# The output projection of a group by Strassen's seven products, and weights in rings of blocks

## The chip, the cores and the metric

The kernel runs on one core of a Trainium2 chip. The metric is the device time of one execution in microseconds (us), as the median of several runs. A profile is one execution, recorded instruction by instruction. The engines are TensorE (PE; its weight loads are shown as PEld), VectorE (DVE), ScalarE (ACT), GpSimd (POOL) and SyncE (SP). SP and POOL issue the transfers (DMA) here. Matmuls write into PSUM; the kernel uses eight banks of it, four for projections and output products, two for scores, two for the attention products.

## The reference

The input x has 8 sequences of 256 tokens with 512 features, in float32, as everything is.

```python
xn = layernorm(x)
q = rope(xn @ wq.T)            # 32 heads of 128
k = rope(xn @ wk.T)            # 8 key/value heads, each used by 4 query heads
v = xn @ wv.T
scores = q @ k.T / sqrt(128)   # scaled by key for later query rows, then causal
s = concat_heads(softmax(scores) @ v) @ wo.T       # (256, 4096) @ (4096, 512)
g = silu(top-2 of 4 low-rank experts of xn)
out = x + s * g
```

## The kernel before

The tokens are worked in NTB = 4 token blocks of two sequences (512 tokens, b = 0 and 1). A token block has eight groups g, one for each key/value head with its four query heads. A *step* is one group of one token block (32 steps), a *unit* one group of one sequence (64 units).

**Projections.** q, k and v are made in *quads*: 512 output features by 512 input features for both sequences, by Strassen's method in the form of Winograd: seven products of half-size blocks in place of eight. A product is a `piece` of `quad`, four matmuls of 256 columns (eight instructions in the profile, since a float32 matmul is two). Its weight operand is one of the four blocks A11, A12, A21, A22 or of their sums S1 to S4, its other operand a block or a sum of the activations (XB, XT). The products go into three PSUM banks (pa, pd, pe) and are put together by VectorE and ScalarE, which keep intermediate values in "side" tiles. There are twelve quads a token block.

`load_weights` brings the weights of a quad. In the first token block it loads the four blocks, VectorE forms the three further sums and S3 (S3 takes the place of A21), and POOL writes all seven to a scratch tensor in DRAM; later blocks read all seven from there in one transfer. The tile of seven blocks has two buffers.

**Attention.** `softmax` of a unit makes scores with TensorE, exponentials with ScalarE and normalising with VectorE, in one buffer p; VectorE transposes 32 by 32 blocks, and a bounce through DRAM (spread, then gather: `there`, `pT`, issued by SP) completes the transposition. `values` multiplies pT with v: av, for a half t of the query rows and all four heads, 512 columns wide. ScalarE copies it to aT.

**Output.** `load_out_weights` brings the 512 by 512 part of wo of a group, one tile of two buffers. `out_project` makes, for each t, `po`: four matmuls of 512 columns (one for a head), then VectorE adds the bank to the sum s of that row block (the first group copies). After the last group `finish` multiplies by the gate, adds x and stores. The gates are made by `experts` early in each token block and stay in four tiles.

**Order.** The program is written as jobs with engines, estimated durations, predecessors and buffers (*holds*). TensorE's jobs are laid in an order that weaves the quads of the next step with the scores of a step, the attention products of two units before (LAG_V) and the output products of three units before (LAG_O). `Plan.run` then plays the jobs through with these estimates; on each engine the earliest due job that is ready and has its buffers goes first. The order it finds is the program's order on every engine, and each engine then keeps to it on the chip. A hold with turns (x, w, wo) is taken in the order in which it was asked for. The wait for a result, or for a buffer, stands at the head of the instruction that needs it, and all that is later on the same engine or the same issuing queue is behind it. All engine calls pass through one helper, so nearly every row of the profile names its line, L116; the tiles tell what a row is. The tile names: `paq`, `pdq`, `peq` are the three banks of a query quad (k and v for keys and values), `s` the sums of the output, `w` a quad's weights, `wo` the output weights.

Of the kernel before, what the change touches and what calls it, by code (L numbers as in the profile page):

```python
# [69 lines left out]
A11, A12, A22, S3, S1, S2, S4 = range(7)  # L70
A21 = S3
# [33 lines left out]
class InOrder:  # L105
# [15 lines left out]
    def __init__(self, tc):  # L121
        for name in ("tensor", "vector", "scalar", "gpsimd", "sync"):
            setattr(self, name, self.Engine(tc, getattr(tc.nc, name)))

# [124 lines left out]
def layer(ctx: ExitStack, tc: tile.TileContext, x, wquad, woT, raT, bT, table, out):  # L249
# [6 lines left out]
    four = pool("four", 4)  # L256
# [12 lines left out]
        store.tile([P, 7, 2 * 2 * P], F32, tag=f"sums{i}", name=f"sums{i}") for i in range(NQUAD)  # L269
    ]  # L270

# [5 lines left out]
    def hold(tag):  # L277
        return Hold(rooms[tag])

    for tag, n in dict(  # L280
        mm=4, sc=2, av=2, x=4, m=2, s=4, gates=4, side=3, w=2, wo=2, c=2, sw=2, qT=3, kk=3, v=3,
        z=2, p=1, blocks=1, pT=3, aT=4, X=1,
    ).items():
        rooms[tag] = Room(n, tag in ("x", "w", "wo"))
# [3 lines left out]
    gates, sums_of, acts, out_weights, weights, x_hold = {}, {}, {}, {}, {}, {}  # L288
# [3 lines left out]
    def norm(tb):  # L292
# [4 lines left out]
        xh = [hold("x") for _ in range(NT)]  # L297
# [4 lines left out]
        def load(t):  # L302
            xs[t] = four.tile([P, D], F32, tag="x", name=f"x{tb}_{t}")
            nc.sync.dma_start(out=xs[t], in_=x[bass.ds(tb * TB + t * P, P), :])
# [46 lines left out]
        issues = [add("sp", 0.3, lambda t=t: load(t), opens=[xh[t]]) for t in range(NT)]  # L351
# [13 lines left out]
        for t in range(NT):  # L365
            xn = add("dve", 0.4, lambda t=t: normalise(t), after=[done[t]], opens=[mh[t]], closes=[xh[t]])
# [17 lines left out]
    def load_weights(tb, quad, first):  # L384

        h = hold("w")
        n = f"{tb}_{quad}"
        box = {}
        flat = lambda i, j: sums[quad][:, i:j, :].rearrange("p i (c m) -> p i c m", c=2)

        def load():
            w = box["w"] = two.tile([P, 7, 2, 2 * P], F32, tag="w", name=f"w{n}")
            if tb:
                nc.gpsimd.dma_start(out=w, in_=flat(0, 7))
            else:
                (nc.sync if first else nc.gpsimd).dma_start(out=w[:, :4], in_=wquad[quad])

        def form(i):
            w = box["w"]
            a, b, c, op = (  # L400
                (A21, A22, S1, nc.vector.tensor_add),
                (S1, A11, S2, nc.vector.tensor_sub),
                (A11, A21, S3, nc.vector.tensor_sub),
                (A12, S2, S4, nc.vector.tensor_sub),
            )[i]
            op(w[:, c], w[:, a], w[:, b])

        def keep_sums():
            nc.gpsimd.dma_start(out=flat(0, 7), in_=box["w"])

        if tb:
            there = add(
                "pool", 0.7, load, opens=[h], after=[sums_of[quad]], lag=9.0
            )
            return box, h, [there] * 7
        there = add(
            "sp" if first else "pool", 0.7, load, opens=[h], after=first, lag=11.0 if first else 7.0
        )
        f1 = add("dve", 0.7, lambda: form(0), after=[there])
        f2 = add("dve", 0.7, lambda: form(1), after=[f1])  # L420
        f3 = add("dve", 0.7, lambda: form(2), after=[f1])
        f4 = add("dve", 0.7, lambda: form(3), after=[f2])
        sums_of[quad] = add(
            "pool", 0.7, keep_sums, after=[f3, f4], closes=[h], lag=7.0
        )
        return box, h, [there, there, there, f3, f1, f2, f4]

    def quad(tb, which, out, room, rows, name):
# [3 lines left out]
        wbox, wh, there = load_weights(tb, which, [] if len(weights) > 1 else begun)  # L432
# [8 lines left out]
        def product(bank, i, half, b, t, first):  # L441
            w = wbox["w"]
# [5 lines left out]
            for m in range(2):  # L448
                for c in range(2):
                    a, x_ = w[:, i, c, :], xb[:, c, :]  # L450
# [7 lines left out]
        def piece(bank, i, half, b, t, first, after):  # L458
# [4 lines left out]
                closes=[wh, x_hold[tb]],  # L463
# [15 lines left out]
        if not tb:  # L479
            sums_of[which].near = (p1, 0.0)  # L480
# [264 lines left out]
    def values(tb, g, b):  # L745
# [5 lines left out]
        def of(t):  # L751
            box = {}

            def work():
                v = vbox[b][:, :, bass.ts(g % G, HD)]
                av = box["av"] = ps_av.tile([P, G, P], F32, tag="av", name=f"av{n}_{t}")
                for k in range(t + 1):
                    nc.tensor.matmul(
                        av, lhsT=v[:, k, :], rhs=pbox["pT"][:, :, t + k, :], start=k == 0,
                        stop=k == t,  # L760
                    )

            def read():
                box["aT"] = four.tile([P, G, P], F32, tag="aT", name=f"aT{n}_{t}")
                nc.scalar.copy(box["aT"], box["av"])

            h, ah = hold("av"), hold("aT")
            av = add(
                "pe", 0.86 * (t + 1), work, after=[p_done] + v_done, opens=[h], closes=[ph, vh]
            )  # L770
            aT = add("act", 0.6, read, after=[av], opens=[ah], closes=[h], near=(av, 1.0))
            attn[tb, g, 2 * b + t] = box, ah, aT
            pieces.append(av)

        for t in range(2):
            of(t)
        return pieces


    def load_out_weights(tb, g):  # L780
# [312 lines left out]
```

## Time and profile before

| what | value |
|---|---|
| runs | 1411.73, 1414.01, 1414.49 us; median 1414.01 |
| the profiled execution | 1410.33 us, span 1408.5 us, 15988 instructions |
| PE, PEld | 1384.1 us (98%), 952.8 us (68%) |
| DVE | 951.4 us (68%) |
| ACT | 604.3 us (43%) |
| POOL | 57.7 us (4%) |
| DMA | 249.31 MB, 177 GB/s on the mean |

The span runs from the first to the last instruction of the profiled execution; the execution takes 1.8 us more. A row of the groups reads: line, engine, operation, output <- inputs, shape, count | busy us in total, mean ns of one | idle us of the engine just before them <- what ended it. In the list of waits a row is: who waited for whom, us in total, times, the longest. In a timeline a row is: start in us, us, engine, line, operation and count. Ends of matmuls are modelled, so their durations overlap and the distance from start to start is what one costs. A DMA row gives the queue that issues, count, size, and the median us from issue to landing.

### The profile page before, as it was taken

The page shows a single profiled execution, that of the slowest core. Times are in us where ns is not written, and L with a number is a line of the kernel's source. Part 1 is how long each engine was busy: PE and PEld are TensorE (multiplying, and loading weights), DVE is VectorE, ACT ScalarE, POOL GpSimd, SP SyncE. Part 2 cuts the span into 40 slices and gives each one's busy share as a digit, 9 for nine tenths or more (in the row PEclk, how much of TensorE's full clock was granted, in tenths as well). Part 3 has the DMA queues.
Part 4 walks back from the last instruction along what each step waited for, and adds up shares of the span by engine and source line. Part 5 has one row for each costly group of instructions (what it writes and reads, how often), then busy time and mean ns, then how long its engine had stood idle before and what let it go on. Part 6 is the DMA issues. An engine that isn't in the chain of part 4 may idle for free.

```text
span 1408.5 us, 15988 instructions
## 1 busy us (share of the span) xinstructions
PE 1384.1 (98%) x5360; PEld 952.8 (68%) x5360; DVE 951.4 (68%) x2566; ACT 604.3 (43%) x1559; POOL 57.7 (4%) x97
## 2 busy tenths in 40 slices
PE   6999999999999999999999999999999999999998
PEld 5866676667766677666776766766677766676653
DVE  5888677776677657577485765847767666665663
ACT  3444444453534435344443444435444344434521
POOL 1000000000000000000000000000000000000000
PEclk9999999999999999999999999999999999999999
DMA  5667556655465553554655554555546454454453
GB/s 217 231 225 257 193 184 230 234 172 167 154 209 171 172 160 128 184 190 161 194 181 179 153 165 152 184 174 166 158 164 227 162 171 143 153 199 127 135 157 97
DMA packets 71170, 249.31 MB, mean 177 GB/s; under 512 B 7920, under 2 KB 40688, under 8 KB 63408
## 3 DMA queue, kind: packets, MB, share of 16 engines
q1 hardware_dynamic: 53280, 115.37, 27.4%
q0 software_dynamic: 17056, 132.13, 25.7%
q8 instruction: 42, 0.69, 0.2%
q10 hardware_dynamic: 752, 0.80, 0.2%
q14 instruction: 40, 0.33, 0.1%
HBM read 171.72 MB, written 76.55 MB: 176 GB/s over the span
## 4 chain that ended last, share of the span: by engine, by line
PE 94%; DMA 4%; DVE 2%; SPq 0%; issue 0%; ACT 0%; DVEq 0%
PE po L116 29%; PE paq L116 15%; PE av L116 11%; PE sc L116 9%; PE pdq L116 8%; PE pav L116 4%; PE pak L116 4%; PE peq L116 4%; DMA there<-blocks 2%; PE pdv L116 2%; PE pdk L116 2%; DMA pT<-there 1%; PE dle L116 1%; PE lme L116 1%; PE pev L116 1%; PE pek L116 1%
## 5 line engine op out<-in xcount | busy, mean ns | idle before, releaser
L116 PE MATMUL po<-wo,aT 128*128 128x512 f32 x1024 | 463.8, 596 | 0.0
L116 PEld LDWEIGHTS po<-wo,aT 128*128 128x128 f32 x1024 | 188.9, 191 | 194.9 <-issue 192.7
L116 ACT ACTIVATE p<-z,least 128x256 f32<-128x256 f32 (+7 forms) x512 | 207.4, 407 | 163.7 <-DVE least L116 150.9
L116 DVE CUSTOM_DVE_ANT_0 z<-sc,tab 128x256 f32<-128x256 f32 (+7 forms) x512 | 136.4, 304 | 164.6 <-PE sc L116 147.2
L116 PE MATMUL av<-pT,v 128*128 128x512 f32 x384 | 188.0, 602 | 8.0 <-DMA pT<-there 8.0
L116 PEld LDWEIGHTS sc<-kk,qTq 128*128 128x128 f32 x1024 | 163.8, 191 | 43.1 <-issue 31.1
L116 PE MATMUL paq<-XT,w 128*128 128x256 f32 x768 | 183.4, 382 | 0.2 <-ACT u3q L116 0.2
L116 PE MATMUL sc<-kk,qTq 128*128 128x256 f32 (+7 forms) x1024 | 172.8, 302 | 0.0
L116 PEld LDWEIGHTS paq<-XT,w 128*128 128x128 f32 x768 | 143.6, 190 | 42.4 <-issue 24.0
L116 DVE TENSOR_TENSOR s<-s,po 128x512 f32<-128x512 f32 x112 | 76.6, 684 | 119.9 <-PE po L116 119.7
L116 ACT COPY aT<-av 128x512 f32<-128x512 f32 x128 | 74.6, 583 | 150.2 <-PE av L116 149.8
L116 ACT COPY swq<-cq 64x1024 f32<-64x1024 f32 x128 | 133.6, 1044 | 7.4 <-DVE qTq L116 5.1
L116 DVE STREAM_TRANSPOSE blocks<-p 128x1024 f32<-128x1024 f32 (+1 forms) x128 | 123.2, 967 | 0.5 <-issue 0.2
L116 DVE TENSOR_SCALAR p<-p,total 128x256 f32<-128x256 f32 (+7 forms) x512 | 117.2, 293 | 2.3
L116 PEld LDWEIGHTS av<-pT,v 128*128 128x128 f32 x384 | 72.6, 192 | 54.3 <-issue 41.8
L116 ACT ACTIVATION_READ_ACCUMULATOR p<-z,least 128x1 f32 x512 | 96.1, 188 | 0.0
L116 DVE TENSOR_TENSOR qTq<-cq,tab 128x1024 f32<-128x1024 f32 x64 | 78.1, 1220 | 22.3 <-ACT cq L116 22.3
L116 DVE TENSOR_TENSOR qTq<-qTq,swq 128x1024 f32<-128x1024 f32 x64 | 77.7, 1215 | 0.5
L116 DVE TENSOR_TENSOR swq<-swq,tab 128x1024 f32<-128x1024 f32 x64 | 77.9, 1217 | 0.0
L116 PE MATMUL paq<-XB,w 128*128 128x256 f32 x256 | 61.1, 381 | 0.0
L116 PEld LDWEIGHTS pdq<-XT,w 128*128 128x128 f32 x256 | 48.6, 190 | 18.5 <-issue 11.7
L116 PE MATMUL pdq<-XT,w 128*128 128x256 f32 x256 | 60.6, 379 | 0.0
(106 smaller groups left out, 1329.1 us busy)
## 6 DMA issues: line engine op xcount, KB each, us to landing
w<-sums POOLq DMA_DIRECT2D x36, 1792.0 KB, 7.7
there<-blocks SPq DMA_DIRECT2D x256, 192.0 KB, 3.3
pT<-there SPq DMA_DIRECT2D x64, 768.0 KB, 4.3
wo<-in_woT_dram POOLq DMA_DIRECT2D x32, 1024.0 KB, 9.2
sums<-w POOLq DMA_DIRECT2D x12, 1792.0 KB, 7.5
w<-in_wquad_dram POOLq DMA_DIRECT2D x10, 1024.0 KB, 5.1
x<-in_x_dram SPq DMA_DIRECT2D x16, 256.0 KB, 5.3
xf<-in_x_dram SPq DMA_DIRECT2D x16, 256.0 KB, 4.7
```

Of the source, the lines that this page charges most:

```text
L116: ins = what(*args, **kwargs)
```

## The change

Four things change.

1. The output product of a step (both sequences of a group) is done as a quad is: 2 by 2 blocks of the attention output (rows: sequences, columns: pairs of heads) with 2 by 2 blocks of the output weights (rows: pairs of heads, columns: halves of the 512 features), by seven products. `values` therefore makes av by pair of heads k, all 256 query rows in one tile, with matmuls of 256 columns. VectorE forms four sums of attention blocks in each step (`s` and, in place, `a` in the new names), and four sums of output weights in each step of the first token block.
2. Each of the seven products has a sum of its own, `acc` 1 to 7, over the eight groups. The first group copies with ScalarE, the others add with VectorE. Only after the last group `finish` puts the seven together to the four blocks of the output, in seven additions, and then gates, adds x and stores, each block of two row tiles by 256 columns.
3. Weights come in blocks of 256 KB, each a tile of its own, in rings of 9 places (quads) and 8 places (output weights). Blocks are taken in turn and released one by one. In the first token block the four sums are formed into places of the ring and each is written to DRAM by a transfer of its own; later blocks load three blocks from the weights and four sums from the scratch tensors.
4. The gates are written to DRAM by SP and read back before the end of the token block, and x is loaded in pairs of row tiles.

A step's seven products are split in the order of the work: two are laid at the end of the step after their group's, five in the step after that (`held`). In the lines below a product's number is that of its sum.

```diff
-A11, A12, A22, S3, S1, S2, S4 = range(7)
-A21 = S3
+A11, A12, A22, A21, S1, S2, S4 = range(7)
+S3 = A21
+ACC, RING, RING_O, RING_A, XPAIRS = 8, 9, 8, 9, 2
...
-        mm=4, sc=2, av=2, x=4, m=2, s=4, gates=4, side=3, w=2, wo=2, c=2, sw=2, qT=3, kk=3, v=3,
-        z=2, p=1, blocks=1, pT=3, aT=4, X=1,
+        mm=4, sc=2, av=2, x=XPAIRS, m=2, acc=ACC, side=3, w=RING, wo=RING_O, a=RING_A, c=2, sw=2, qT=3,
+        kk=3, v=3, z=2, p=1, blocks=1, pT=3, X=1,
     ).items():
-        rooms[tag] = Room(n, tag in ("x", "w", "wo"))
+        rooms[tag] = Room(n, tag in ("x", "w", "wo", "a", "acc"))
...
-        wbox, wh, there = load_weights(tb, which, [] if len(weights) > 1 else begun)
+        wbox, wh, there = blocks_of(
+            tb, "w", w_pool, wquad[which], sums[which], which, Features,
+            [] if len(weights) > 1 else begun,
+        )
...
-        def of(t):
+        def of(k):
+            heads = slice(2 * k, 2 * k + 2)
             box = {}
             def work():
                 v = vbox[b][:, :, bass.ts(g % G, HD)]
-                av = box["av"] = ps_av.tile([P, G, P], F32, tag="av", name=f"av{n}_{t}")
-                for k in range(t + 1):
+                pT = pbox["pT"][:, heads]
+                av = box["av"] = ps_av.tile([P, 2, 2, P], F32, tag="av", name=f"av{n}_{k}")
+                for t, block, keys_ in ((0, 0, 0), (1, 1, 0), (1, 2, 1)):
                     nc.tensor.matmul(
-                        av, lhsT=v[:, k, :], rhs=pbox["pT"][:, :, t + k, :], start=k == 0,
-                        stop=k == t,
+                        av[:, :, t, :], lhsT=v[:, keys_, :], rhs=pT[:, :, block, :],
+                        start=block == 0, stop=block != 1, skip_group_check=True,
                     )
             def read():
-                box["aT"] = four.tile([P, G, P], F32, tag="aT", name=f"aT{n}_{t}")
-                nc.scalar.copy(box["aT"], box["av"])
...
-            h, ah = hold("av"), hold("aT")
-            av = add(
-                "pe", 0.86 * (t + 1), work, after=[p_done] + v_done, opens=[h], closes=[ph, vh]
-            )
-            aT = add("act", 0.6, read, after=[av], opens=[ah], closes=[h], near=(av, 1.0))
-            attn[tb, g, 2 * b + t] = box, ah, aT
+                box["a"] = a_pool.tile([P, 2, S], F32, tag="a", name=f"a{n}_{k}")
+                nc.scalar.copy(box["a"], box["av"].rearrange("p h t q -> p h (t q)"))
+            h, ah = hold("av"), hold("a")
+            av = add("pe", 1.3, work, after=[p_done] + v_done, opens=[h], closes=[ph, vh])
+            a = add("act", 0.6, read, after=[av], opens=[ah], closes=[h], near=(av, 1.0))
+            attn[tb, g, b, k] = box, ah, a
             pieces.append(av)
-        for t in range(2):
-            of(t)
+        for k in range(2):
+            of(k)
         return pieces
...
         def silu(t):
-            h = hold("gates")
+            h = hold("m")
...
-                mine["w"] = four.tile([P, O], F32, tag="gates", name=f"gates{n}_{t}")
+                mine["w"] = two.tile([P, O], F32, tag="m", name=f"gates{n}_{t}")
                 nc.scalar.activation(mine["w"], mine["dl"], AF.Tanh, scale=0.5)
...
             d = add("dve", 0.7, whole, after=[a], closes=[dh], near=(p, 2.0))
-            gates[tb, t] = mine, h, d
+            gates[tb].append(
+                add(
+                    "sp", 0.3, lambda: nc.sync.dma_start(out=gates_dram[tb][:, t, :], in_=mine["w"]),
+                    after=[d], closes=[h], near=(p, 4.0), lag=4.0,
+                )
+            )
             return p
...
-    LAG_V, LAG_O = 2, 3
+    LAG_V = 2
+    held = []
...
     for n in range(len(steps) + 2):
         last = n >= len(steps)
         tb, g = (NTB, 0) if last else steps[n]
-        (sa, va, oa), (sb, vb, ob) = (
-            (part(softmax, u), part(values, u - LAG_V), part(out_project, u - LAG_O))
-            for u in (NB * n, NB * n + 1)
-        )
-        fill = oa[:1] + va[:1] + sa[:1] + va[1:] + sa[1:2] + oa[1:] + sa[2:]
-        later = [ob[:1], vb[:1], sb[:1], vb[1:], sb[1:2], ob[1:], sb[2:]]
+        (sa, va), (sb, vb) = (
+            (part(softmax, u), part(values, u - LAG_V)) for u in (NB * n, NB * n + 1)
+        )
+        ob = out_project(*steps[n - 1]) if 0 < n <= len(steps) else []
+        oa, held = held, ob[2:]
+        fill = oa[:1] + va[:1] + sa[:1] + oa[1:2] + va[1:] + sa[1:2] + oa[2:4] + sa[2:]
+        later = [oa[4:], ob[:1], vb[:1], sb[:1], ob[1:2], vb[1:], sb[1:2], sb[2:]]
```

The new functions, as they stand in the changed kernel (in the diff `blocks_of` takes the place of `load_weights`, and `out_project` and `finish` those of the same names and of `load_out_weights`):

```python
def blocks_of(tb, room, ring, source, kept, key, form, first):
    n = f"{room}{tb}_{key}"
    box, there, holds = {}, {}, {}
    order = (A11, A21, A22, A12, S1, S2, S4) if not tb else form.order
    def load(i):
        w = box[i] = ring.tile([P, 2, 2 * P], F32, tag=room, name=f"{n}_{i}")
        k = form.sums.index(i) if tb and i in form.sums else None
        src = source[:, i] if k is None else kept[:, k].rearrange("p (c m) -> p c m", c=2)
        (nc.sync if first else nc.gpsimd).dma_start(out=w, in_=src)
    def sum_up(i):
        to, a, b, op = form.steps[i]
        if to not in box:
            box[to] = ring.tile([P, 2, 2 * P], F32, tag=room, name=f"{n}_{to}")
        getattr(nc.vector, op)(box[to], box[a], box[b])
    def keep_sum(i):
        k = form.sums.index(i)
        nc.gpsimd.dma_start(
            out=kept[:, k].rearrange("p (c m) -> p c m", c=2), in_=box[i]
        )
    for i in order:
        holds[i] = hold(room)
    if tb:
        for i in order:
            after = [sums_of[room, key, i]] if i in form.sums else []
            there[i] = add("pool", 0.8, lambda i=i: load(i), after=after, opens=[holds[i]], lag=4.5)
        return box, holds, there
    issue = list(first)
    for i in order[:4]:
        there[i] = add(
            "sp" if first else "pool", 0.4 if first else 0.8, lambda i=i: load(i), after=issue,
            opens=[holds[i]], lag=10.0 if first else 4.5,
        )
    for i, (to, a, b, op) in enumerate(form.steps):
        there[to] = add(
            "dve", 0.7, lambda i=i: sum_up(i), after=[there[a], there[b]] + form.before(i, there),
            opens=[holds[to]] if to in order[4:] else [], closes=[holds[a], holds[b]],
        )
    for i in form.sums:
        sums_of[room, key, i] = add(
            "pool", 0.8, lambda i=i: keep_sum(i), after=[there[i]], closes=[holds[i]],
            lag=5.0,
        )
    return box, holds, there
class Features:
    order = (A11, A12, S2, S1, S3, A22, S4)
    sums = (S1, S2, S3, S4)
    steps = (
        (S1, A21, A22, "tensor_add"), (S2, S1, A11, "tensor_sub"),
        (S3, A11, A21, "tensor_sub"), (S4, A12, S2, "tensor_sub"),
    )
    @staticmethod
    def before(i, there):
        return [there[S1]] if i == 2 else []
class Outputs:
    order = (A11, A21, S2, S1, A12, S4, A22)
    sums = (S1, S2, A12, S4)
    steps = (
        (S1, A12, A11, "tensor_sub"), (S2, A22, S1, "tensor_sub"),
        (A12, A22, A12, "tensor_sub"), (S4, A21, S2, "tensor_sub"),
    )
    @staticmethod
    def before(i, there):
        return [there[S1]] if i == 2 else []
...
def out_project(tb, g):
    n = f"{tb}_{g}"
    wbox, wh, w_done = blocks_of(
        tb, "wo", wo_pool, woquad[g], out_sums[g], g, Outputs, []
    )
    abox, ah, a_done = {}, {}, {}
    for i, (b, k) in {A11: (0, 0), A12: (0, 1), A21: (1, 0), A22: (1, 1)}.items():
        abox[i], ah[i], a_done[i] = attn.pop((tb, g, b, k))
    def sum_up(i):
        to, a, b, op = Features.steps[i]
        if to not in abox:
            abox[to] = {"a": a_pool.tile([P, 2, S], F32, tag="a", name=f"s{n}_{to}")}
        getattr(nc.vector, op)(abox[to]["a"], abox[a]["a"], abox[b]["a"])
    for i in (S1, S2, S4):
        ah[i] = hold("a")
    p21 = a_done[A21]
    for i, (to, a, b, op) in enumerate(Features.steps):
        a_done[to] = add(
            "dve", 0.7, lambda i=i: sum_up(i),
            after=[a_done[a], a_done[b]] + Features.before(i, a_done),
            opens=[ah[to]] if to != S3 else [], closes=[ah[a], ah[b]],
        )
    pieces = {}
    def product(k, a, w):
        box = {}
        def work():
            ps = box["ps"] = ps_mm.tile([P, 2, 2 * P], F32, tag="mm", name=f"po{n}_{k}")
            for t in range(2):
                for h in range(2):
                    nc.tensor.matmul(
                        ps[:, t, :], lhsT=abox[a]["a"][:, h, bass.ts(t, P)],
                        rhs=wbox[w][:, h, :], start=t == h == 0, stop=h == 1,
                        skip_group_check=True,
                    )
        def add_up():
            if g == 0:
                s = acc[tb, k]["s"] = acc_pool.tile(
                    [P, 2, 2 * P], F32, tag="acc", name=f"acc{tb}_{k}"
                )
                nc.scalar.copy(s, box["ps"])
            else:
                s = acc[tb, k]["s"]
                nc.vector.tensor_add(s, s, box["ps"])
        h = hold("mm")
        p = add("pe", 1.73, work, after=[a_done[a], w_done[w]], opens=[h], closes=[ah[a], wh[w]])
        if g == 0:
            acc[tb, k] = {"hold": hold("acc"), "done": None}
        mine = acc[tb, k]
        mine["done"] = add(
            "act" if g == 0 else "dve", 0.7, add_up, after=[p, mine["done"]], closes=[h],
            opens=[mine["hold"]] if g == 0 else [], near=(p, 1.0),
        )
        mine["last"] = p
        pieces[k] = p
    for k, a, w in (
        (1, A11, A11), (2, A12, A21), (6, S2, S2), (5, S1, S1), (7, S3, A12), (4, A22, S4),
        (3, S4, A22),
    ):
        product(k, a, w)
    if not tb:
        for i in Outputs.sums:
            sums_of["wo", g, i].near = (pieces[1], 0.0)
    if g == KV - 1:
        finish(tb)
    return [pieces[k] for k in (1, 2, 6, 5, 7, 4, 3)]
def finish(tb):
    M = {k: acc[tb, k] for k in range(1, 8)}
    def put(to, a, b, closes=()):
        near = max((M[a]["last"], M[b]["last"]), key=lambda p: p.number)
        M[to]["done"] = add(
            "dve", 0.7, lambda: nc.vector.tensor_add(M[to]["s"], M[a]["s"], M[b]["s"]),
            after=turn + [M[to]["done"], M[a]["done"], M[b]["done"]], closes=[M[k]["hold"] for k in closes],
            near=(near, 2.0),
        )
        M[to]["last"] = near
        turn[:] = [M[to]["done"]]
    loads, turn = {}, []
    def inputs(b):
        box = {}
    ...
        pl, tag = (two, "c") if b and tb == NTB - 1 else (x_pool, "x")
        xh, gh = hold(tag), hold(tag)
        rows = x[bass.ds(tb * TB + b * S, S), :].rearrange("(t p) o -> p t o", p=P)
        def load(what):
            box[what] = pl.tile([P, 2, D], F32, tag=tag, name=f"{what}{tb}_{b}")
            src = rows if what == "xf" else gates_dram[tb][:, bass.ts(b, 2), :]
            nc.sync.dma_start(out=box[what], in_=src)
        near = (M[2]["last"], -12.0)
        done = [
            add("sp", 0.3, lambda: load("g"), after=gates[tb][2 * b : 2 * b + 2], opens=[xh],
                near=near, lag=5.0),
            add("sp", 0.3, lambda: load("xf"), opens=[gh], near=near, lag=5.0),
        ]
        loads[b] = box, [xh, gh], done
    def result(k, b, f):
        box, holds, done = loads[b]
        s = lambda: M[k]["s"]
        cols = bass.ts(f, 2 * P)
        rows = out[bass.ds(tb * TB + b * S, S), cols].rearrange("(t p) o -> p t o", p=P)
        near = M[k]["last"]
        m = add(
            "dve", 0.7, lambda: nc.vector.scalar_tensor_tensor(
                s(), s(), 0.5, box["g"][:, :, cols], op0=ALU.mult, op1=ALU.mult
            ),
            after=[M[k]["done"], done[0]], closes=[holds[0]], near=(near, 3.0),
        )
        a = add(
            "dve", 0.7, lambda: nc.vector.tensor_add(s(), s(), box["xf"][:, :, cols]),
            after=[m, done[1]], closes=[holds[1]], near=(near, 4.0),
        )
        add(
            "sp", 0.3, lambda: nc.sync.dma_start(out=rows, in_=s()), after=[a],
            closes=[M[k]["hold"]], near=(near, 5.0), lag=4.0,
        )
    inputs(0)
    put(2, 1, 2)
    result(2, 0, 0)
    put(1, 1, 6, [6])
    put(7, 1, 7)
    put(1, 1, 5)
    put(5, 7, 5)
    put(4, 7, 4, [7])
    put(3, 1, 3, [1])
    result(3, 0, 1)
    inputs(1)
    result(5, 1, 1)
```

## The prediction

> **What bounds the kernel now.** I read the busy shares first, then what TensorE waits for, then the stretches by token block, then single rows.
>
> ```profile
> PE 1384.1 (98%) x5360; PEld 952.8 (68%) x5360; DVE 951.4 (68%) x2566; ACT 604.3 (43%) x1559; POOL 57.7 (4%) x97
> ...
> PE 94%; DMA 4%; DVE 2%; SPq 0%; issue 0%; ACT 0%; DVEq 0%
> ```
>
> TensorE is busy for 1384 of 1408.5 us and holds 94% of the chain that ended last. A busy PE need not be an efficient one, but here the matmuls stand back to back, so less matmul time shortens the kernel until something else is late. The waits of TensorE:
>
> ```profile
> PE xp L116 <- DVE xn L116: 8.6, 2, 7.0
> PE av L116 <- DMA pT<-there: 8.0, 4, 3.0
> PE xp L116 <- DVE rstd L116: 2.2, 1, 2.2
> ```
>
> Nearly all are start-up (xp) and four late landings of pT, two of them at the end. In between nothing is late. VectorE stands next. The first line below is the first token block from 50 us on, the second the second block, the third the densest 20 us:
>
> ```profile
> 50.00:345.00 295.00, 291.45 (x1147) 203.96 (x1146) 220.31 (x586) 134.33 (x355) 15.95 (x27) 1.00 0.63 214
> ...
> 345.00:689.00 344.00, 344.00 (x1342) 237.40 (x1341) 230.21 (x629) 151.25 (x389) 12.38 (x20) 1.00 0.52 171
> ...
> 70.00:90.00 20.00, 17.33 (x88) 14.84 (x86) 19.23 (x57) 10.32 (x25) 1.29 (x2) 1.00 0.78 281
> ```
>
> The columns are length, PE, weight loads, DVE, ACT, POOL, granted clock, DMA share, GB/s. VectorE has 220 of 295 us (75%), later 230 of 344 (67%). Between 70 and 90 us it is at 96%, and there TensorE stands for 2.7 us: the softmax is late, so pT is.
>
> **TensorE: what is removed.** The timeline gives the real pitch, which is shorter than an instruction's recorded duration:
>
> ```profile
> 341.01 3.60 PE L116 MATMUL po<-wo,aT 128*128 128x512 f32 x8
> ...
> 344.45 1.89 PE L116 MATMUL peq<-XB,w 128*128 128x256 f32 x8
> 346.17 1.03 PE L116 MATMUL paq<-XT,w 128*128 128x256 f32 x4
> ```
>
> (The last line is cut by the stretch asked for; its start is what counts.) A product po of eight 512-column instructions takes 344.45 - 341.01 = 3.44 us; a Strassen piece of eight 256-column ones 346.17 - 344.45 = 1.72 us, 215 ns each, with its 190 ns weight loads under it. Before, each of the 32 steps (4 token blocks, 8 groups) has four po: 13.76 us. After, it has seven products of the same form as a quad's piece: 7 x 1.725 = 12.08. The gain is 32 x 1.68 = 53.9 us. The attention product av goes from 6 instructions of 512 columns a unit to 12 of 256: 6 x 0.430 = 2.58 against 12 x 0.215 = 2.58, nothing.
>
> **VectorE: what is added.**
>
> ```profile
> L116 DVE TENSOR_TENSOR s<-s,po 128x512 f32<-128x512 f32 x112 | 76.6, 684 | 119.9 <-PE po L116 119.7
> L116 DVE TENSOR_TENSOR w<-w 128x512 f32<-128x512 f32 x48 | 31.2, 683 | 1.7 <-DMA w<-in_wquad_dram 1.6
> ```
>
> All new operations have these forms, 0.684 us (where two follow each other in the timeline, 0.61). Sums of the attention blocks: 4 x 32 = 128. Products added up: 7 x 28 = 196 in place of 112 + 16 copies, 68 more (the first group's 28 copies go to ACT: 28 x 0.585 = 16 us there, at 43%). Putting together: 7 x 4 = 28. Sums of output weights, first block only: 32. That is 256 x 0.684 = 175 us, so VectorE comes to some 1126 us of 1370, 82%.
>
> By block: a later one gets (32 + 17 + 7) x 0.684 = 38 us: 268 of 344 - 13.5 = 330.5, 81%. Before, TensorE loses nothing at 67 to 75%; I take 1 us a block, 3 in all (ends 0 and 15). The first block, 50 to 345 us, gets 32 + 28 + 14 = 74 operations, 45 to 51 us: 265 to 271 of 291.5 - 7 x 1.68 = 279.7 us of TensorE work. That is 95 to 97%, the load at which TensorE stood between 70 and 90 us. If VectorE runs at 93% there (between the 85% of 50 to 90 us and the 96%), the stretch takes 268 / 0.93 = 288 us. 279.7 plus the 3.5 it already stands is 283, so +5; with up to 1 us at the start, where the second quad's last blocks wait for places of the first's, +6. Ends: 0 (96%), and +22 (88%: 305).
>
> **Weights in rings.**
>
> ```profile
> w<-sums POOLq DMA_DIRECT2D x36, 1792.0 KB, 7.7
> ...
> x<-in_x_dram SPq DMA_DIRECT2D x16, 256.0 KB, 5.3
> ```
>
> Loads of 1 and 1.75 MB become blocks of 256 KB; POOL issues about 575 transfers in place of 90, at the 0.53 us of its present issues 305 us, a queue less than a quarter full. It is in order: a block's load that waits for TensorE to leave a place holds the later blocks and the kept sums behind it, and SP's first loads likewise. But with 9 places (8 for the output weights) and 7 blocks to a quad, a place comes free seven or eight products before its next block is used. Even back to back, seven pieces take 7 x 1.72 = 12 us, against 5.3 + 0.5 for the block. Cost 0 while this cover stands; without it each block would cost up to 5.8 us. The Trainium skill (DMA: Bandwidth & Descriptors) speaks against the change: gather transfers to 1 MiB or more for three quarters of peak (section Bandwidth), and its fit of 2.0 us plus the bytes over 436 GB/s (section Anatomy of one DMA) makes one load of a whole quad 6.2 us but seven of 256 KB, one after the other, 18: by it, as an estimate, 12 us more a quad, over 400 us for the 36 quads that load seven, if nothing hid it. By the rows 5.3 us a block, which overlap and lie a step ahead: 0. I take the rows, since volume is no bound: some 26 MB more than 249 (output weights +27, gates +8, quads -9), DMA share 0.52 to about 0.59. SP gets 16 stores and 8 loads of gates among its bounces; by the row above they land in some 5 us, and are wanted later than that.
>
> **The end.**
>
> ```profile
> 1393.50 2.84 PE L116 MATMUL av<-pT,v 128*128 128x512 f32 x6 [1.59 <-DMA pT<-there]
> 1396.18 7.03 PE L116 MATMUL po<-wo,aT 128*128 128x512 f32 x16
> ...
> 1404.69 0.69 DVE L116 TENSOR_TENSOR s<-s,xf 128x512 f32<-128x512 f32 x1
> ...
> 1370.00:1375.00 5.00, 5.00 (x7) 1.90 (x8) 0.52 (x6) 1.55 (x5) 0.00 (x0) 0.50 0.61 170
> ```
>
> From the last pT to the end is 1408.5 - 1393.5 = 15.0 us: av, two po, three VectorE operations, 3.1 us of store. After: av 2.6, copy and hop 0.8, five of the seven products 8.6, ten VectorE operations that the built order puts behind the last product (it adds it up, then puts together and gates three results) 6.6, store 3.1: 21.7, so +6.7. Three more additions stand between the last softmax's scaling and its transposes: +2. The last line shows that after a gap of 2.9 us the clock fell to 0.50 (its av took 5.49 in place of 2.74); such a gap may go, or come again before the last av. I take +9 in all (+3 to +15).
>
> **Sum.** -53.9 + 6 + 3 + 9 = -36 against the profiled execution of 1410.3 us (span 1408.5, 1.8 around it): 1374.4. The runs' median, 1414.0, lies 3.7 above it, so **1378**.
>
> **Rivals.** (1) VectorE becomes the bound: the first block runs at 88% and the others lose 5 us each: -53.9 + 22 + 15 + 12 = -5, 1409; it spans 1390 to 1411. For it: 95 to 97% wanted, in an engine that keeps its order; against: the later blocks have a fifth to spare. (2) Slower: the new sums of attention blocks wait on VectorE for av, and so for pT. When pT is late, all behind them stands: the additions that free the four PSUM banks (a quad holds three) and the next scores. Then each late pT makes the next. It decides once a step loses 36 / 32 = 1.2 us more; at 1.5 us the time is 1378 + 48 = 1426. For it: four late pT before; against: 8.0 us in all of them, and the VectorE share. (3) The narrow products don't run as the quads' pieces do: at 1.88 us in place of 1.725, 224 x 0.155 = 35 us are gone and it is 1413, no change. Against: 1.72 in every quad.
>
> **Numbers.** The likeliest case, 1364 to 1390, 0.68; better still 0.04; rival 1 0.15 (0.01 of it no change); rival 2 0.10; rival 3 0.03. 0.2% is 2.8 us, about what a measurement tells from no change here. Faster 0.68 + 0.04 + 0.14 = 0.86, same 0.04, slower 0.10. The range 1364 to 1406 leaves out the best 0.04, a fifth of rival 1 (0.03), and rivals 2 and 3: 0.20.
>
> **What would show it.** po in 1792 instructions of 256 columns, 8 of them in 1.72 us; VectorE near 1126 us and over 90% busy from 50 to 330 us; TensorE's new waits there on VectorE or pT, a few us; none on w or wo; 20 us or more from the last pT to the end. The prediction is wrong if a later block takes over 335 us, or if TensorE waits for weight blocks.

## The result and the profile after

The changed kernel takes 1391.01 us as the median of four runs (1387.08 to 1394.26), the kernel before 1413.55 (1411.73 to 1414.49): a ratio of 0.984 (95% interval 0.9805 to 0.9876). That is 22.5 us less, within the predicted range, but 13 us above the predicted 1378. The profiled execution took 1394.26 us, with a span of 1391.5 us where before had 1408.5. It is the slowest of the four, and the profiled one of before, at 1410.33, was faster than its own median, so what the two traces differ by (17.0 us) is less than what the medians do; a reading of a few us from one pair of traces has to be taken with that.

The page of the changed kernel, its busy shares and its chain of work that ended last:

```profile
PE 1340.2 (96%) x6512; PEld 1175.7 (84%) x6512; DVE 1102.4 (79%) x2822; ACT 614.2 (44%) x1587; POOL 313.8 (23%) x579
...
PE 83%; DMA 10%; DVE 4%; SPq 1%; issue 1%; ACT 0%; DVEq 0%; ACTq 0%
```

TensorE works 43.9 us less (1384.1 - 1340.2), but the span is only 17.0 us shorter: idle time rose from 24.4 to 51.3 us. The chain says where to look. Transfers hold 10% of it in place of 4%, VectorE only 4%. What TensorE waited for, again of the changed kernel (us in total, times, the longest):

```profile
PE av L118 <- DMA pT<-there: 25.3, 13, 3.6
PE xp L118 <- DVE xn L118: 12.8, 4, 8.0
PE po L118 <- ACT a L118: 1.4, 2, 0.7
PE sc L118 <- DVE least L118: 0.8, 1, 0.8
PE sc L118 <- DVE qTq L118: 0.5, 1, 0.5
PE xp L118 <- DVE cq L118: 0.3, 1, 0.3
```

Before, pT was late four times, for 8.0 us. Now it is late thirteen times, for 25.3. The start (xp) costs 12.8 us where it took 10.8. No row has `w` or `wo` as what was waited for, and beyond the start VectorE keeps TensorE waiting for 1.6 us in all. The transfers of the changed kernel (queue, count, size, median us from issue to landing):

```profile
there<-blocks SPq DMA_DIRECT2D x256, 192.0 KB, 3.6
pT<-there SPq DMA_DIRECT2D x64, 768.0 KB, 5.7
...
w<-sums POOLq DMA_DIRECT2D x144, 256.0 KB, 3.8
```

The gather of the kernel before:

```profile
pT<-there SPq DMA_DIRECT2D x64, 768.0 KB, 4.3
```

The gather pT, whose instruction did not change, lands in 5.7 us where it took 4.3 before; the spread in 3.6 where it took 3.3. The kernel moves 275.80 MB in place of 249.31, and the DMA share of a later block (the second line below) is 0.65 where it was 0.52. The windows of the changed kernel, with the columns as in the prediction's windows:

```profile
50.00:330.00 280.00, 272.65 (x1310) 238.68 (x1309) 245.50 (x627) 130.58 (x345) 73.53 (x136) 0.98 0.69 213
680.00:1015.00 335.00, 329.33 (x1620) 289.79 (x1619) 261.88 (x684) 153.82 (x396) 75.14 (x138) 1.00 0.65 200
105.00:108.00 3.00, 2.99 (x7) 2.45 (x8) 0.00 (x0) 0.02 (x1) 0.03 (x1) 0.50 0.79 219
```

The third line belongs to one of the thirteen waits. In TensorE's timeline it reads:

```profile
105.01 2.93 PE L118 MATMUL av<-pT,v 128*128 128x256 f32 x6 [3.60 <-DMA pT<-there]
...
1025.30 1.46 PE L118 MATMUL av<-pT,v 128*128 128x256 f32 x6
...
1028.00 1.97 PE L118 MATMUL paq<-XB,w 128*128 128x256 f32 x8
1032.96 2.90 PE L118 MATMUL av<-pT,v 128*128 128x256 f32 x6 [2.99 <-DMA pT<-there]
...
1367.28 4.50 PE L118 MATMUL av<-pT,v 128*128 128x256 f32 x12 [3.58 <-DMA pT<-there]
...
1377.73 1.89 PE L118 MATMUL po<-wo,a 128*128 128x256 f32 x8
1379.46 1.89 PE L118 MATMUL po<-wo,s 128*128 128x256 f32 x8
```

After the gaps shown here six instructions of av take 2.9 us; otherwise they take 1.46, as at 1025.30. The granted clock from 105 to 108 us is 0.50. Of the thirteen waits the five longest (2.57 to 3.60 us) were followed by such a spell, the eight others (0.60 to 2.36) were not. So a late pT can cost twice, as a wait and as matmuls at half speed, and the second part hides in "busy". In its five spells TensorE was busy for 19.2 us at 0.50, a loss of some 9.6. In the second case SP had issued pT at 1026.18 us, and behind it, within 0.9 us, the 512 KB of gates that the change reads back and 512 KB of x; TensorE could begin 6.8 us after the issue.

By token block, from one first router product (`lme`) to the next, the last to the end of the span:

| kernel | to block 2 | block 2 | block 3 | block 4 and end |
|---|---|---|---|---|
| before | 431.3 | 344.05 | 344.05 | 289.1 |
| after | 426.2 | 335.4 | 339.4 | 290.5 |
| gained | 5.1 | 8.6 | 4.7 | -1.4 |
| the prediction's sum | 7.5 | 12.5 | 12.5 | 3.5 |

(The last row is 13.5 a block from TensorE less the stalls: 6 in the first, 1 in each other, and 9 at the end.) Every stage fell short.

### The profile page after: what moved, and what is told of

The parts are those of the page before. It is cut to its first block, busy times and chain, and to the rows that moved or that the text cites. A ratio compares the mean times of both kernels' runs of the same rounds, so it can differ in the third digit from the quotient of the medians.

```text
span 1391.5 us, 19888 instructions
## 1 busy us (share of the span) xinstructions
PE 1340.2 (96%) x6512; PEld 1175.7 (84%) x6512; DVE 1102.4 (79%) x2822; ACT 614.2 (44%) x1587; POOL 313.8 (23%) x579
## 2 busy tenths in 40 slices
DMA packets 106134, 275.80 MB, mean 198 GB/s; under 512 B 15985, under 2 KB 52849, under 8 KB 106033
## 4 chain that ended last, share of the span: by engine, by line
PE 83%; DMA 10%; DVE 4%; SPq 1%; issue 1%; ACT 0%; DVEq 0%; ACTq 0%
PE po L118 23%; PE paq L118 13%; PE av L118 11%; PE sc L118 9%; PE pdq L118 7%; DMA pT<-there 6%; PE pak L118 4%; PE pav L118 4%; DMA there<-blocks 4%; PE peq L118 3%; PE pdk L118 2%; PE pdv L118 2%; DVE acc L118 1%; PE dle L118 1%; PE pev L118 1%; PE lme L118 1%
## 5 line engine op out<-in xcount | busy, mean ns | idle before, releaser
L118 PE MATMUL po<-wo,a 128*128 128x256 f32 x1024 | 241.2, 380 | 1.4 <-ACT a L118 1.4
L118 PE MATMUL av<-pT,v 128*128 128x256 f32 x768 | 194.1, 393 | 25.3 <-DMA pT<-there 25.3
L118 PEld LDWEIGHTS po<-wo,a 128*128 128x128 f32 x1024 | 192.2, 190 | 26.0 <-ACT a L118 2.6
L118 PEld LDWEIGHTS av<-pT,v 128*128 128x128 f32 x768 | 149.5, 197 | 50.7 <-issue 14.4
L118 PE MATMUL po<-wo,s 128*128 128x256 f32 x768 | 182.7, 382 | 0.0
L118 DVE TENSOR_TENSOR acc<-acc,po 128x512 f32<-128x512 f32 x196 | 132.9, 678 | 46.7 <-PE po L118 44.8
L118 ACT COPY a<-av 128x512 f32<-128x512 f32 x128 | 73.9, 581 | 213.0 <-PE av L118 213.0
L118 PEld LDWEIGHTS po<-wo,s 128*128 128x128 f32 x768 | 145.2, 191 | 24.1 <-issue 5.3
L118 POOL DMA_DIRECT2D w<-sums x144 | 78.9, 548 | 361.0 <-PE paq L118 139.3
L118 POOL DMA_DIRECT2D w<-in_wquad_dram x148 | 81.0, 549 | 252.4 <-PE paq L118 87.8
```

What stands on the lines that cost most here:

```text
L118: ins = what(*args, **kwargs)
```

## The experiments

Two theories stood against each other. **A:** the blocks of weights that now come all through a step make the bounce slower, and pT comes later than the order reckons with. **B:** VectorE, with its added work, makes the softmax late, and pT with it. The ratios below are to the kernel before, timed beside each, with the 95% interval.

### VectorE relieved: narrow_acc

```diff
-nc.vector.tensor_add(s, s, box["ps"])
+nc.vector.tensor_add(s[:, :, :32], s[:, :, :32], box["ps"][:, :, :32])
```

> The 196 additions of products to their sums work on 32 of 256 columns only (so the output leaves most of the sum out); jobs, estimates and order are those of the changed kernel, and every transfer too. VectorE loses 196 x about 0.5 = 100 us. Theory A (the transfers: pT lands late because POOL's blocks are nearly always in flight beside it, median landing 5.7 us in place of 4.3): the landing stays at 5.7, TensorE's waits for pT stay near 25 us, time 1384 to 1391. Theory B (VectorE at 79%: the softmax is finished late): the waits fall below 10 us, time 1370 to 1378, landing as it is.

Measured: 0.985 (0.9828 to 0.9875), the same as the change itself. The page of narrow_acc:

```profile
PE 1337.9 (97%) x6512; PEld 1175.7 (85%) x6512; DVE 1015.2 (73%) x2822; ACT 614.4 (44%) x1587; POOL 314.2 (23%) x579
```

And its waits:

```profile
PE av L118 <- DMA pT<-there: 22.0, 12, 3.5
```

87 us less work on VectorE leave twelve late pT where there were thirteen. Between 50 and 330 us its share falls from 88% to 83%, and TensorE's busy time there stays at 272 us. B falls, as far as these additions go; some 64 of the 151 us that the change added to VectorE are still there. The gather landed in 5.4 us, where 5.7 was expected, with every transfer and the order as in the change: 0.3 us between two medians is no difference to build on.

### Fewer transfers: half_wo and quarter_wo

```diff
-wbox, wh, w_done = blocks_of(tb, "wo", ...)
+if tb and g % 2:
+    wbox, wh, w_done = shared.pop()
+else:
+    wbox, wh, w_done = blocks_of(tb, "wo", ...)
+    if tb:
+        shared.append((wbox, wh, w_done))
```

> In the second to fourth token block an odd group uses the output weight blocks of the group before it (wrong weights, so the output is not the reference's); 12 groups load nothing, 22 MB of 276 less. VectorE's work is unchanged. Theory A: the landing of pT falls to about 5.3 us, some of TensorE's waits for it go, 3 to 6 us faster than the changed kernel (1385 to 1388). Theory B: within 3 us of the changed kernel, 1388 to 1394.

Measured: 0.980 (0.9776 to 0.9823), 1378.92 us. The waits of half_wo:

```profile
PE av L118 <- DMA pT<-there: 13.8, 8, 4.1
```

By the ratio that is 6 us less than the change, whose interval it overlaps, and on the same chip 9.0 less than narrow_acc (1387.96), whose interval it does not, with VectorE as busy as ever (1102.6 us). Only POOL issues less; on the other engines and on SP everything stands in the order of the change. Against the trace of the change 11.5 us of waits for pT are gone, and 4.3 of busy TensorE (1335.9) at a granted clock of 0.994 in place of 0.990. The gather's own median, 5.3 us, is not told from narrow_acc's 5.4, but the bounce as a whole is shorter: from the first spread's issue to the gather's landing it takes 11.4 us at the median, where it takes 12.0 in narrow_acc, 12.2 in the change and 9.5 before. A stands. quarter_wo goes further, with three of four groups reusing (`g % 4`, `shared[-1]`):

> The changed kernel with its own estimates; in the second to fourth token block three groups of four use the output weight blocks of the group before them (wrong weights): some 33 MB less than 276, so a little less than the kernel before moves. If bytes alone delay pT, its landing is back at 4.3 us and the waits at 8 us or less, time 1366 to 1374 (with clock drops gone). If it is that blocks come spread over the step, the landing stays near 4.9 as with rings alone (240 MB), waits about 10 us, time 1374 to 1380.

Measured: 0.976 (0.9738 to 0.9785), 1377.79 us; pT lands in 5.2 us (the bounce in 11.3) and is late six times, for 13.1 us. It moves 242.75 MB, less than the kernel before, whose pT took 4.3 us. So the bytes alone are not the reason.

### The order told the truth: late_pT

The planner reckons 4 us for the spread and 5 for the gather. The gather kept that before (4.3 at the median; 7 of the 64 took over 5.0 us) and breaks it now (5.7; 42 of 64). late_pT changes only these two estimates: the same instructions, and the same 275.80 MB, in another order.

```diff
-out_ = add("sp", 1.4, spread, after=[t1], closes=[bh], near=(sc, 9.0), lag=4.0)
-in_ = add("sp", 0.35, gather, after=[out_], opens=[th], lag=5.0)
+out_ = add("sp", 1.4, spread, after=[t1], closes=[bh], near=(sc, 9.0), lag=5.0)
+in_ = add("sp", 0.35, gather, after=[out_], opens=[th], lag=8.0)
```

> Only the planner's estimates change: the bounce's first leg 5.0 in place of 4.0 us, the second 8.0 in place of 5.0. Same instructions, other order. If the waits for pT are a matter of how late the order asks for it (A and B both allow that), most of the 25 us of waits in the first three and a half blocks go and the clock drops that follow them: 1374 to 1382. If pT cannot be had earlier, since VectorE is full (the strong form of B), other waits take their place: 1386 to 1394.

Measured: 1367.59 us (1365.85 to 1374.24), 0.972 (0.969 to 0.9745). The page of late_pT, and its waits:

```profile
PE 1330.1 (97%) x6512; PEld 1170.3 (86%) x6512; DVE 1099.7 (81%) x2822; ACT 612.9 (45%) x1587; POOL 313.9 (23%) x579
```

```profile
PE av L118 <- DMA pT<-there: 5.1, 2, 2.7
```

Its gather, and its window from 50 to 330 us:

```profile
pT<-there SPq DMA_DIRECT2D x64, 768.0 KB, 5.4
```

```profile
50.00:330.00 280.00, 276.70 (x1351) 242.72 (x1350) 249.64 (x639) 135.13 (x361) 75.85 (x141) 1.00 0.70 218
```

pT still takes 5.4 us, but av now stands late enough in the order. Such an order cures a late pT whatever made it late, so this run shows what the lateness costs, not where it comes from. By the ratios it is 1.2% below the change, 17 us. Between the two traces the span is 26.8 us shorter (1364.7): 16.7 of idle time and 10.1 of TensorE's busy time, for the same matmuls at a granted clock of 0.998 in place of 0.990. TensorE's busy time is now 54.0 us below before's. In the first block VectorE is busy 89% of the stretch (249.64 of 280) and TensorE 99%. The stages are 417.4, 332.2, 332.1 and 283.0 us: 14.0, 11.9, 11.9 and 6.1 less than before.

Two neighbours show how much of it is needed. leg2 changes the gather's estimate alone, to 6.5; later has 6.0 and 11.0.

> The changed kernel with one estimate of the planner raised: the bounce's second leg 6.5 in place of 5.0 us (the measured landings of pT are 5.7 at the median, 7.6 at most); the first leg stays at 4.0. If the loss is this one estimate, which the landing of before (4.3) kept and the new one does not, most of what 5.0 and 8.0 gave (a ratio of 0.9718 to the kernel before) is there already: 0.972 to 0.977, waits for pT under 10 us. If it takes the wider margin on both legs: 0.978 to 0.984.

> The estimates 6.0 and 11.0: still wider. If 5.0 and 8.0 already cover the landings (9.1 us at most), no more is gained: ratio 0.970 to 0.974; the last steps, where there is little other work, may lose 2 to 4 us.

Measured: leg2 0.977 (0.9751 to 0.9792), between its two forecasts, with a landing of 6.1 us and nine late pT for 12.9; later 0.970 (0.968 to 0.9718), no late pT at all, and no gain over late_pT that the intervals can tell. leg2 gives about half (0.7% of 1.2%); from 5.0 and 8.0 to 6.0 and 11.0 nothing more is gained.

### Was it in the kernel before too: before_late, rings_only, rings_late

before_late is the kernel before with the estimates of late_pT. rings_only is the kernel before with its quads' weights in a ring of nine blocks (`blocks_of` in place of `load_weights`), and its output products as they were; rings_late has both.

> Control: the kernel before with the estimates that helped the changed one (5.0 and 8.0). Its order already waits only 8.0 us for pT, 4.5 of it in the last 40 us, so by theory A at most 3 to 8 us faster: ratio 0.994 to 0.998. If the order as such were the gain, it would be far more (0.98).

> The kernel before with the ring of 9 blocks for the quads alone; output products as before. Theory A: the landing of pT rises from 4.3 us towards 5, with some new waits: 1413 to 1420. Theory B: VectorE has the work of before, so 1411 to 1416 and a landing of 4.3.

> The kernel before with the ring for the quads and the estimates 5.0 and 8.0: what the ring is worth once pT is on time. The ring alone gave 0.9962, the estimates alone 0.9942; if they save different things (the first block's loads, and the end) they add to 0.990 to 0.992, if both save the same waits it stays at 0.993 to 0.995.

Measured: before_late 0.994 (0.9927 to 0.9957), with one late pT (2.5 us); rings_only 0.996 (0.9947 to 0.9978); rings_late 0.992 (0.99 to 0.9931), near the product of the two, 0.990. The transfers and the waits of rings_only:

```profile
pT<-there SPq DMA_DIRECT2D x64, 768.0 KB, 4.9
```

```profile
PE av L117 <- DMA pT<-there: 3.9, 2, 2.2
```

So the ring alone, with 240 MB moved, already lengthens the gather, from 4.3 to 4.9 us (4.5 in rings_late); 30 and 25 of the 64 take over 5.0 us, where it was 7. Yet the new waits that A led to expect did not come, and the kernel is a little faster. The wider estimates were worth 0.6% before the change and 1.2% after it. Set beside rings_late, late_pT has the output products by seven and their own weight blocks as what is left: 0.972 / 0.992 = 0.980, some 28 us.

Why a landing of 4.9 us did no harm there, and 5.7 did in the change, is seen in the room that the order leaves. Here the room is the time from the issue of the first spread to the first matmul of av, and the bounce the time from that issue to the gather's landing; both are medians taken from the traces, and where pT was late the room includes the wait.

| kernel | room, first sequence of a step | room, second | bounce | late pT |
|---|---|---|---|---|
| before | 16.2 | 21.5 | 9.5 | 4 |
| rings_only | 16.2 | 21.5 | 10.7 | 2 |
| after | 13.6 | 19.7 | 12.2 | 13 |
| leg2 | 13.9 | 19.7 | 12.5 | 9 |
| late_pT | 16.8 | 20.2 | 12.3 | 2 |
| later | 20.6 | 21.0 | 12.1 | 0 |

So the change squeezed pT from both sides: the bounce became 2.7 us longer, and the room about 2 us shorter. A step of TensorE's work is 1.7 us shorter, which would bring av nearer to its softmax; no run parts that from the rest of the new order. As an estimate from the trace of the change: with gathers of at most 4.3 us in the same order six of the waits would be left, 8.0 us of the 25.3.

### Is it the size of the transfers: before_w7

The kernel before, with each load of 1.75 MB issued as seven of 256 KB, one behind the other:

```diff
-nc.gpsimd.dma_start(out=w, in_=flat(0, 7))
+for i in range(7):
+    nc.gpsimd.dma_start(out=w[:, i : i + 1], in_=flat(i, i + 1))
```

> The kernel before, with each load of seven blocks of a quad split into seven transfers of 256 KB, issued one after the other into the same tile: the same bytes at nearly the same time, in shorter runs. If what delays pT is the form of the transfers (runs of 2 KB), its landing rises from 4.3 to about 4.9 as with rings alone. If it is that they are spread over the step, so that nearly every pT meets one, it stays at 4.3 to 4.5. Time 1405 to 1413 beside a kernel before of 1409 either way.

Measured: 1415.0 us, 1.0018 (1.0007 to 1.0029), at most 0.3% slower. The transfers of before_w7:

```profile
pT<-there SPq DMA_DIRECT2D x64, 768.0 KB, 4.3
...
w<-sums POOLq DMA_DIRECT2D x252, 256.0 KB, 4.6
```

252 blocks of 256 KB leave pT at 4.3 us when they come in bunches. Neither their size nor the number of issues on POOL's queue by itself delays it. What is left is that the ring's blocks come one at a time, all through the step, as places come free, so that a gather meets some of them more often. The issues and landings in the traces bear this out. In before, and in before_w7, 53 of the 64 gathers met no transfer of POOL's between issue and landing, and these took 4.26 us at the median. In rings_only only 19 met none, and they took 4.26 us too; the 45 others took 5.5. In the change all but one met some. How they and a gather get in each other's way inside the DMA engines no run here shows.

### What is left on VectorE and at the end: late_narrow, late_tail

late_narrow is late_pT with the narrow additions. late_tail is late_pT with one of the last block's four results put together and gated by GpSimd, with one operation on ScalarE.

> The order of the estimates 5.0 and 8.0 with the 196 additions on 32 of 256 columns (most of the sum is left out): VectorE 87 us less, all else the same. If VectorE's load still costs TensorE time once pT is no longer late, this is 5 us or more faster than with the full additions (ratio 0.968 or less). If VectorE at 81% costs nothing but the end, 1 to 2 us: ratio 0.970 to 0.972.

> The changed kernel with the estimates 5.0 and 8.0, and in the last token block one of the four results put together, gated and added on GpSimd and ScalarE in place of VectorE. VectorE has ten operations of 0.61 us behind the last product; three fewer give 1.8 us if GpSimd's chain is done by then. 0 to 2 us faster than without (ratio 0.970 to 0.972); slower by some us if GpSimd takes over 1.5 us for an operation.

Measured: late_narrow 0.969 (0.9674 to 0.9706) and late_tail 0.971 (0.9693 to 0.9727): with late_pT's interval of 0.969 to 0.9745, neither is told from it. The 87 us on VectorE cost nothing that can be measured, even at 89%. The tail did not shorten either: from the last addition of a product to the end of the span late_tail takes 1369.7 - 1358.50 = 11.2 us, late_pT 1364.7 - 1354.89 = 9.8. The last operations of late_tail in its timeline:

```profile
1357.94 1.76 POOL L118 TENSOR_TENSOR acc<-acc,acc 128x512 f32<-128x512 f32 x1 [18.90 <-DVE acc L118]
1358.50 0.68 DVE L118 TENSOR_TENSOR acc<-acc,po 128x512 f32<-128x512 f32 x1
1359.10 1.16 DVE L118 TENSOR_TENSOR acc<-acc,acc 128x512 f32<-128x512 f32 x1
1359.78 1.59 POOL L118 TENSOR_TENSOR acc<-acc,g 128x512 f32<-128x512 f32 x1
1360.29 1.63 DVE L118 SCALAR_TENSOR_TENSOR acc<-acc,g 128x512 f32<-128x512 f32 x1
...
1362.12 1.53 POOL L118 TENSOR_TENSOR acc<-acc,xf 128x512 f32<-128x512 f32 x1 [0.74 <-ACT acc L118]
1362.45 1.75 DVE L118 TENSOR_TENSOR acc<-acc,xf 128x512 f32<-128x512 f32 x1
```

GpSimd takes 1.5 to 1.8 us for what VectorE does in 0.68, and VectorE's own operations stretch beside it, to 1.16, 1.63 and 1.75 us.

A kernel with the seven output products but with whole quads in one transfer, which would part the two halves of the change most directly, was not tried.

## Why the prediction came out as it did

The measured 1391.0 us lies in the stated range, but past the likeliest case (1364 to 1390), in the stretch that the range owed to rival 1; that case did not come about, so that the number fell inside is in part luck. The mechanism was right for the matmuls and wrong for the transfers: the second and third blocks took 335.4 and 339.4 us, past the 335 that the prediction had named as the sign of being wrong.

- **TensorE, -53.9: right within some 3 us.** po is 1792 instructions of 256 columns, and a product takes 1.73 us (1377.73 to 1379.46 in the last step). With the half-clock spells gone, late_pT's busy time is 54.0 us below before's; some 3 of that are before's own half-clock av (5.49 us in place of 2.74, in the prediction's last lines), so the matmuls alone give some 51. In the change itself 10.1 were paid back, nearly all as matmuls at half clock, for which the sum had no term.
- **"Cost 0 while this cover stands" and "volume is no bound": this step failed.** It asked only whether a block of weights would come too late for its product. None did, as predicted, and as 256 KB transfers they cost next to nothing (before_w7); the Trainium skill's rule of 1 MiB and more (DMA: Bandwidth & Descriptors, section Bandwidth), beside which the prediction worked out over 400 us from the page's fit, decided nothing here. The step did not ask what the blocks do to a transfer that others wait for, nor what a shorter step leaves of its room. The gather went from 4.3 to 5.7 us, past the 5.0 on which the order rests, the room shrank by about 2 us, and 8.0 us of waits became 25.3. It could have been seen beforehand: four pT were late already, and between the row's 4.3 and the 5.0 in the code lay 0.7 us. The DMA share of a later block also came to 0.65, above the 0.59 foreseen.
- **"+6" for the first block and "1 us a block" for the later ones, both laid to VectorE: the wrong engine.** VectorE came to 1102.4 us where 1126 was foreseen (additions that follow each other cost 0.61, as the prediction's own row had it), and to 88% between 50 and 330 us where over 90% was foreseen. Taking 87 us off it changed nothing, before the order was mended or after (narrow_acc, late_narrow). The losses against 13.5 us a block were 8.4 in the first, 4.9 in the second and 8.8 in the third, and the second and third gained 3.2 and 7.2 of it back when only the place of av in the order was changed.
- **"+9" at the end: too small by a few us.** From the last pT to the end it was 1391.5 - 1367.28 = 24.2 us in place of 15.0: 9.2 more, against 6.7 for the same stretch in the sum. The ten VectorE operations behind the last product came as foreseen, from 1381.72 us on. But the gap before the last av came again (3.58 us), and its twelve instructions took 4.50 us in place of 2.6. The last block's stage lost 14.9 us against 13.5 less, where 10 was foreseen; that part of it lies before the last pT was not taken apart.
- **The rivals.** Rival 2, where each late pT makes the next, came half true: pT was late thirteen times and a later block took 339.4 us, past the 335 named as the sign. But its cause was not VectorE and it did not chain: 51 of the 64 pT were in time. Rival 1 would have landed near the measured time for the wrong reason: 1391.01 lies in its span of 1390 to 1411. Rival 3 is refuted by the pitch.

By the traces the change is thus the matmuls' -54, +10 in slower matmuls and +27 in idle time (51.3 against 24.4): -17.0, where the medians say -22.5. Of the 37 lost, the trace of late_pT has 26.8 back. That version, at 0.972, beats both kernels.

## What to carry to other kernels

Before new transfers are costed as hidden, look up the transfer with the least slack and ask what more traffic, spread evenly, does to its landing, and what shorter work in front of its user leaves of its room; here 2.7 us on a bounce of 9.5 and some 2 us less room were enough. Where a planned order rests on estimates, compare each with its landing time after the change: two corrected numbers gave 1.2%, and taking 87 us off an engine that was busy for 88% of a stretch gave nothing. A late operand costs more than its wait where the clock falls after the gap, so look for the half-speed instructions behind it.

## What was not expected of the hardware

- In the change five waits of TensorE, of 2.57 to 3.60 us, were followed by some 3.4 us at a granted clock of 0.50 (6.8 after the longest), and av took 2.5 to 2.9 us in place of 1.46. But not each wait of that length was: in half_wo the row below ran at a granted clock of 1.00, and so did av after 2.99 us in before and 2.73 in late_pT. The Trainium skill (TensorE: Matmul & The Clock Gate, Part 1) tells of a free-running window of about 3.4 us; here a gap of 2.57 us was enough once, and one of 3.54 was not.

```profile
319.42 1.56 PE L118 MATMUL av<-pT,v 128*128 128x256 f32 x6 [3.54 <-DMA pT<-there]
```

- Small transfers in a bunch did not disturb most of the 768 KB gathers (4.3 us with 249.36 MB); blocks spread over the step did (4.5 and 4.9 us with 239.95 MB, 5.2 with 242.75, 5.4 to 6.1 with 275.80).
- In late_tail's last operations VectorE stood still beside GpSimd only where both its inputs lay in SBUF. The one addition with a PSUM input (`acc<-acc,po`, at 1358.50) took 0.68 us while GpSimd was at work, but each of the three others that began while a GpSimd operation ran ended some 0.55 us after that operation had (1360.26 after 1359.70, 1361.92 after 1361.37, 1364.20 after 1363.65), as if it ran only then. The Trainium skill (SBUF — State Buffer, section Who interferes with whom) states just this for two SBUF inputs, and these rows agree.
